# Second attention of a two-layer kernel: which turned tiles travel through DRAM, and in which order the tiles of a chunk are made and read

## The chip, the cores and the metric

The kernel runs on one core of one Trainium2 chip. The metric is the device time of one execution in microseconds; the time given is the median of several executions. One execution was also taken with the hardware profiler, and every duration below comes from that one.

## The reference

The input `x` is 8 x 128 x 48 x 48 in float32: 8 images, 128 channels, N = 48 x 48 = 2304 positions, which are the tokens.

```python
x = x + conv_attn(group_norm(x))                 # first attention, masked
t = to_tokens(x)                                  # 8 x 2304 x 128
t = t + full_attn(layer_norm(t))                  # second attention
t = t + ffn(layer_norm(t))                        # batch norm, recurrent scan
```

The first attention projects `x` and 32 channels of position encodings to `q`, `k` and `v` (a leaky ReLU each), multiplies with a lower triangular mask, takes the softmax, and multiplies with `v`. The second has no projections. With `h = layer_norm(t)` it is

```python
attn = softmax(h @ h.T)          # 2304 x 2304 for each image
out  = attn @ h
```

so `h @ h.T` is symmetric, and the change rests on that symmetry. The last part computes `h @ W.T`, normalises it over all images and tokens, and runs `y = sigmoid(wx + y @ V.T)` along the tokens.

## The kernel before

**Tiles.** Everything is float32. The 2304 tokens of an image ("batch" below) are 18 blocks of 128, or NQ = 6 chunks of 384 = QB x 128 (QB = 3). One score tile is 128 keys by 384 queries. For each batch the kernel does the group norm, the projections (L895, L898), the first attention chunk by chunk (`Causal`: scores L1032, exponential L1034, mask on GpSimd L1037, product L1043), then the second attention chunk by chunk (`Full`). The scan (L1601) follows once, after all 8 batches.

**The second attention.** After each chunk of the first attention a small chain of steps makes the normalised tokens of that chunk: `tb` is transposed on TensorE (L953) and copied by ScalarE into `xh` (L1124), channels by tokens; `xhT` holds them tokens by channels. For chunk j, `Full` accumulates in `o` the products of all 18 blocks of the exponentials with `xhT`. By symmetry only blocks in chunks n >= j are computed. Such an item is "direct": scores on TensorE (L1269), exponential on ScalarE into `p` (L1271), product on TensorE (L1291). A block in a chunk n > j is needed again, transposed, by the later chunk n. So VectorE transposes it in squares of 32 x 32 into a tile `t` of the pool `tpool`, two buffers (L1236). When the three blocks of the pair (j, n) are there, `store` writes the tile to DRAM (`e`, four transfers on SyncE's queue, L1187), in an order that swaps the squares. `load` brings it back into `g` (one transfer on SyncE's queue, pool `gpool`, three buffers, L1179), and chunk n reads it in three "turned" items (product L1279). Inside the chunk's own three blocks the same is done with smaller tiles, "mirrored" items: `tm` is written to DRAM `m` and read back into `gm`, on GpSimd's queue (L1217, L1221; product L1287).

**The order.** `Full.items` lists the items of each chunk: the chunk's own blocks first, then direct and turned items spread evenly, the mirrored items last. In chunk 0 there are 18 direct items and no turned ones; in chunk 1 there are 15 direct and 3 turned ones, the pair (0,1); and so on. The stream of all items is fixed when the program is built. A product follows its scores LAG = 3 items later. The first three items of the first attention of batch b+1 are put among the last items of the second attention of batch b.

**The planner.** Each engine and each queue works in the order in which its instructions are written out. A planner (`Stream`, `Chain`) decides that order when the program is built. It keeps an estimated clock, and `tick` runs each step of a side chain once its estimated inputs are ready. `finish(chain)` writes out all the steps of a chain that are left, and `advance` some of them. `prefetch` writes out a load if fewer than three pairs are loaded ahead and the pair was stored some microseconds earlier, then the stores whose tile is estimated to be ready. `self.pairs` gives the order of the loads: (0,1), (0,2), (1,2), (0,3) and so on, 15 in a batch.

**The rest of SyncE's queue.** After each chunk of the second attention another chain writes the new tokens to DRAM (`t_d`, L1357), and fetches them back as `t2x` (L1361) with `scale` (L1363) for the product `wx` (L1369). The position rows `pb` (L854) and pieces for the scan (`t2l_d`, L1400) go the same way. All transfers of this queue take turns on eight semaphores, so a transfer waits until the one eight before it has landed.

Of the kernel before, what the change touches and what calls it, by code (L numbers as in the profile page):

```python
# [14 lines left out]
F32 = mybir.dt.float32  # L15
# [589 lines left out]
def fast_path(ctx: ExitStack, tc: tile.TileContext, x, pe, w_ffn, out, x_tok, w_qkv, w_pos, v_t, gamma_beta, flag):  # L605
    nc = tc.nc
    B, C, H, W = x.shape
    N = H * W
    P = 128
# [4 lines left out]
    NQ = N // QC  # L614
# [52 lines left out]
    with ExitStack() as actx:  # L667
# [335 lines left out]
        class Causal:  # L1003
# [17 lines left out]

            def begin(self, j, m, first):
                b = self.b
                if first:
                    st.finish(projected[b, j])
                    allowed[b] = j + EARLY
                    following(b)
                    if j == NQ - 1:
                        bounds(b)
                off = self.offset(j, m)  # L1030
                s = psum_s(f"s_{b}_{j}_{m}")
                nc.tensor.matmul(s[:, off:QC], keys[b][:, ts(m, P)], queries[b, j][:, off:], start=True, stop=True)  # L1032
                p = pp.tile([P, QC], F32, tag="p", name=f"p_{b}_{j}_{m}")
                nc.scalar.activation(p[:, off:], s[:, off:QC], AF.Exp, scale=SCALE)  # L1034
                ops = [("ACT", 0.16 + (QC - off) * 0.00085)]
                if m >= QB * j:
                    nc.gpsimd.tensor_mul(p[:, off : off + P], p[:, off : off + P], triu)  # L1037
                    ops.append(("POOL", 0.5))
                return p, st.then(st.spend((QC - off) * US), ops)
# [103 lines left out]
        class Full:  # L1143
# [6 lines left out]
            def __init__(self, b):  # L1150
                self.b = b
                self.tiles, self.stored, self.loaded = {}, {}, {}
                self.pairs = [(i, j) for j in range(NQ) for i in range(j)]
                self.used, self.to_store = 0, deque()

            @staticmethod
            def items():
                chunks = []
                for j in range(NQ):
                    ahead = [("direct", QB * n + g) for n in range(j, NQ) for g in range(QB)]  # L1160
                    turn = [("turned", i, g) for i in range(j) for g in range(QB)]
                    both = [((k + 0.5) / len(ahead), w) for k, w in enumerate(ahead)]
                    both += [((k + 0.5) / len(turn), w) for k, w in enumerate(turn)]
                    order_of = [w for _, w in sorted(both, key=lambda e: e[0])]
                    for own in ahead[QB - 2 :: -1]:
                        order_of.remove(own)
                        order_of.insert(0, own)
                    chunks.append(order_of + [("mirrored", g) for g in range(1, QB)])
                return listed(chunks)
# [3 lines left out]
                return max(0, m - QB * j) * P if m < QB * (j + 1) else 0  # L1173

            def load(self):
                i, j = self.pairs[len(self.loaded)]
                d, _ = self.stored[i, j]
                g = gpool.tile([P, R, QB, QB, SQ], F32, tag="g", name=f"g_{self.b}_{i}_{j}")
                nc.sync.dma_start(g.rearrange("p a j m r -> p (a j m r)"), d.rearrange("p a f -> p (a f)"))  # L1179
                self.loaded[i, j] = g  # L1180

            def store(self):
                j, n, t, at = self.to_store.popleft()
                d = dpool.tile([P, R, QB * QB * SQ], F32, tag=f"e_{j}_{n}", name=f"e_{self.b}_{j}_{n}")
                turned = d.rearrange("(b c) a f -> a c b f", b=R)
                for r in range(R):
                    nc.sync.dma_start(turned[r], t[ts(r, SQ)].rearrange("c b j m r -> c b (j m r)"))  # L1187
                self.stored[j, n] = d, max(at, st.now)

            def prefetch(self):  # L1190
                n = len(self.loaded)
                if n < len(self.pairs) and n < self.used + 3 and self.pairs[n] in self.stored:
                    if self.stored[self.pairs[n]][1] + 6.0 <= st.now:
                        self.load()
                while self.to_store and self.to_store[0][3] <= st.now:
                    self.store()

            def mirror(self, j, g, p, ready):

                b, left = self.b, QB - 1 - g  # L1200
                if g == 0:
                    self.tm = chunk_tile("tm", f"tm_{b}_{j}", bufs=1).rearrange("p (b q r) -> p b q r", b=R, q=QB)
                first = g * (QB - 1)
                nc.vector.transpose(  # L1204
                    self.tm[:, :, first : first + left, :].rearrange("p b q r -> p q b r"),
                    p[:, (g + 1) * P :].rearrange("p (q b r) -> p q b r", q=left, b=R),
                )
                at = st.then(ready, [("DVE", 0.17 + left * 0.13)])
                if g < QB - 2:
                    return  # L1210
                gm = chunk_tile("gm", f"gm_{b}_{j}", bufs=1).rearrange("p (a q r) -> p a q r", a=R, q=QB)
                self.gm = gm
                d = dpool.tile([P, R, QB * SQ], F32, tag=f"m_{j % 2}", name=f"m_{b}_{j}")
                tm = self.tm

                def out_of():
                    nc.gpsimd.dma_start(d, tm.rearrange("p b q r -> p b (q r)"))  # L1217

                def back_in():
                    for r in range(R):  # L1220
                        nc.gpsimd.dma_start(  # L1221
                            gm[ts(r, SQ)].rearrange("c a q r -> c a (q r)"), d.rearrange("(a c) b f -> b c a f", a=R)[r]
                        )

                self.moved = st.add([(out_of, 0.0, [("POOL", 1.2), ("", 3.0)]), (back_in, 0.0, [("POOL", 5.0), ("", 3.0)])], at + 0.6 - st.now)
# [18 lines left out]
            def begin(self, j, what, first):  # L1244
# [10 lines left out]
                if what[0] == "turned":  # L1255
                    i, g = what[1:]
                    while (i, j) not in self.loaded:
                        while self.pairs[len(self.loaded)] not in self.stored:
                            self.store()
                        self.load()  # L1260
                    return self.loaded[i, j][:, :, g, :, :].rearrange("p a m r -> p m a r"), 0.0
# [12 lines left out]
            def product(self, j, what, o, p, ready, first, last):  # L1274
                xhT = x_hat[self.b][0]
                if what[0] == "turned":
                    i, g = what[1:]
                    out_ap = o[:, :QC].rearrange("p (m a r) -> p m a r", m=QB, a=R)
                    nc.tensor.matmul(out_ap, xhT[:, QB * i + g, :], p, start=first, stop=last)  # L1279
                    if g == QB - 1:  # L1280
                        self.used += 1
                    cols = QC
                elif what[0] == "mirrored":
# [15 lines left out]
            def after(self, j, o):  # L1299
# [126 lines left out]
                else:  # L1426
                    steps = [
                        (turn_root, 0.0, [("DVE", 0.15)]),
                        (spread, 0.0, [("", 13.0)]),
                        (fetch, 0.0, [("", 9.0)]),  # L1430
                        (product, QC * US, [("DVE", 1.0)]),
                        (stored, 0.0, [("ACT", 0.85)]),
                    ]
# [31 lines left out]
        LAG = 3  # L1465
        stream = []
        for b in range(B):
            part, items = Causal(b), Causal.items()
            if b:

                for k in range(QB):
# [216 lines left out]
```

## Time and profile before

| what | value |
|---|---|
| time, median of 3 | 1742.51 us (1737.38 to 1744.68) |
| the profiled execution | 1747.17 us |
| its span | 1745.5 us |
| TensorE busy | 1705.2 us, 98% |
| VectorE, ScalarE, GpSimd busy | 1190.0, 699.5, 453.9 us |
| moved by DMA | 278.54 MB, 160 GB/s on the mean |
| granted TensorE clock, mean | 0.995 of full |

A row of the groups or of the timeline names engine, line, operation and `out<-in` with the names of the tiles; "L1291 o<-p,xhT" is the product of a direct item. PE is TensorE, PEld its weight load, DVE VectorE, ACT ScalarE, POOL GpSimd, SP SyncE, and SPq the SyncE instructions that issue transfers. A bracket at the end of a row gives the idle time ahead of it and what ended it. Batch b of the second attention starts about 204 us after batch b-1.

### The profile page before, as it was taken

Reading aid. Unit: us, or ns where it says so; the run is one execution under the profiler, and the core shown is the slowest. Engines: PE = TensorE matmul, PEld = TensorE weight load, DVE = VectorE, ACT = ScalarE, POOL = GpSimd, SP = SyncE. Lnnn points to the kernel's source line nnn. Section 1 sums busy time; section 2 is a strip of 40 time slices with the busy share of each in tenths; the row PEclk is TensorE's granted clock in tenths of the full one; section 3 lists DMA queues with packets and bytes.
Section 4 is the critical chain, followed back from the end, with each engine's and each line's share of the span. In section 5 each row is a group of like instructions: output and inputs, shape, how many; then the busy total and the mean of one; then the engine's idle time right before and its main releaser. Section 6 shows DMA issues by size and latency. Waiting matters only on the chain.

```text
span 1745.5 us, 22358 instructions
## 1 busy us (share of the span) xinstructions
PE 1705.2 (98%) x6338; PEld 1094.7 (63%) x6339; DVE 1190.0 (68%) x3259; ACT 699.5 (40%) x1332; POOL 453.9 (26%) x637
## 2 busy tenths in 40 slices
PE   9999999999999999999999999999999999999986
PEld 6666666666666666666666666666666666666565
DVE  5865578656876478755786568864787656864457
ACT  3344334443344423443344433444244432444345
POOL 1232123311233112321224112332123212241206
PEclk9999999999999999999999999999999999999998
DMA  3317763378424874178632784338831686127858
GB/s 120 114 31 213 227 191 100 106 204 235 145 71 138 226 232 112 49 204 230 199 100 81 200 242 144 100 111 230 242 114 55 183 239 198 52 84 205 229 208 219
DMA packets 214697, 278.54 MB, mean 160 GB/s; under 512 B 93889, under 2 KB 178786, under 8 KB 214052
## 3 DMA queue, kind: packets, MB, share of 16 engines
q1 hardware_dynamic: 204396, 255.11, 50.0%
q0 software_dynamic: 9936, 21.51, 4.4%
q8 instruction: 52, 0.85, 0.2%
q14 instruction: 81, 0.66, 0.1%
q10 hardware_dynamic: 232, 0.40, 0.1%
HBM read 157.31 MB, written 119.61 MB: 159 GB/s over the span
## 4 chain that ended last, share of the span: by engine, by line
PE 89%; DMA 5%; DVE 2%; POOL 1%; SPq 1%; issue 1%; ACT 0%; POOLq 0%; DVEq 0%; ACTq 0%
PE s L1032 17%; PE o L1043 17%; PE s L1269 16%; PE o L1291 16%; PE o L1279 10%; DMA g<-e 3%; PE pj L895 3%; PE z L1601 2%; PE o L1287 2%; PE wx L1369 2%; DMA t2x<-t_d 1%; PE pj L898 1%; POOL gm L1221 1%; PE tb L953 1%; PE of_t L953 1%; SPq L1187 1%
## 5 line engine op out<-in xcount | busy, mean ns | idle before, releaser
L1271 ACT ACTIVATE p<-s,shift 128x384 f32<-128x384 f32 (+2 forms) x504 | 274.8, 551 | 544.5 <-PE s L1269 480.1
L1034 ACT ACTIVATE p<-s 128x384 f32<-128x384 f32 (+2 forms) x504 | 230.2, 460 | 395.3 <-PE s L1032 331.2
L1043 PE MATMUL o<-p,vT 128*128 128x384 f32 (+2 forms) x1008 | 377.8, 456 | 4.6 <-POOL p L1037 4.6
L1032 PE MATMUL s<-q,k 128*128 128x384 f32 (+2 forms) x1008 | 381.4, 460 | 0.1
L1269 PE MATMUL s<-xh 128*128 128x384 f32 (+2 forms) x1008 | 378.3, 457 | 0.0
L1291 PE MATMUL o<-p,xhT 128*128 128x384 f32 (+2 forms) x1008 | 367.6, 456 | 0.0
L1279 PE MATMUL o<-g,xhT 128*128 128x384 f32 x720 | 277.7, 489 | 9.7 <-DMA g<-e 9.7
L1236 DVE STREAM_TRANSPOSE t<-p 128x384 f32<-128x384 f32 x360 | 183.9, 550 | 146.3 <-DMA e<-t 75.0
L1291 PEld LDWEIGHTS o<-p,xhT 128*128 128x128 f32 x1008 | 189.2, 190 | 118.8 <-ACT p L1271 0.3
L1043 PEld LDWEIGHTS o<-p,vT 128*128 128x128 f32 x1008 | 186.7, 190 | 115.8 <-POOL p L1037 8.9
L1269 PEld LDWEIGHTS s<-xh 128*128 128x128 f32 x1008 | 184.9, 190 | 105.9
L1032 PEld LDWEIGHTS s<-q,k 128*128 128x128 f32 x1008 | 179.3, 190 | 86.5 <-issue 2.2
L1058 DVE TENSOR_TENSOR acc<-acc,p 128x384 f32<-128x384 f32 (+2 forms) x408 | 209.7, 514 | 26.7 <-DVE acc L1058 1.6
L1279 PEld LDWEIGHTS o<-g,xhT 128*128 128x128 f32 x720 | 131.6, 191 | 89.8 <-DMA g<-e 14.5
L1037 POOL TENSOR_TENSOR p<-p,triu 128x128 f32<-128x128 f32 x144 | 72.2, 505 | 288.7 <-ACT p L1034 287.9
L1221 POOL DMA_DIRECT2D gm<-m x192 | 107.4, 564 | 71.5 <-PE s L1269 25.1
L1128 POOL TENSOR_SCALAR xhT<-xhT 128x384 f32<-128x384 f32 x48 | 57.4, 1195 | 242.4 <-PE tb L953 242.4
L1343 POOL TENSOR_TENSOR roots<-ve_f,mhalf 128x3 f32<-128x3 f32 x48 | 42.3, 880 | 254.8 <-DVE ve_f L937 254.6
L1217 POOL DMA_DIRECT2D m<-tm x48 | 28.9, 602 | 205.4 <-DVE tm L1204 205.0
L1370 DVE TENSOR_TENSOR scale<-wx,scale 128x384 f32<-128x384 f32 x46 | 25.6, 557 | 78.9 <-PE wx L1369 62.9
L895 PE MATMUL pj<-xn,wT 128*128 128x384 f32 x192 | 77.9, 488 | 1.5 <-DVE xn L888 1.5
L902 DVE TENSOR_TENSOR q<-pj,pb 128x384 f32<-128x384 f32 x48 | 26.7, 556 | 69.4 <-PE pj L895 69.4
(248 smaller groups left out, 1732.9 us busy)
## 6 DMA issues: line engine op xcount, KB each, us to landing
e<-t SPq DMA_DIRECT2D x480, 144.0 KB
g<-e SPq DMA_DIRECT2D x120, 576.0 KB
pb<-posb_d SPq DMA_DIRECT2D x42, 576.0 KB
t1t<-in_x_tok_dram SPq DMA_DIRECT2D x48, 192.0 KB
m<-tm POOLq DMA_DIRECT2D x48, 192.0 KB, 4.7
gm<-m POOLq DMA_DIRECT2D x192, 48.0 KB, 3.4
t_d<-tt SPq DMA_DIRECT2D x184, 48.0 KB
t2x<-t_d SPq DMA_DIRECT2D x46, 192.0 KB
```

Source lines behind the costliest of these rows:

```text
L895: nc.tensor.matmul(ps[:, :QC], wT[:, j, :], xn, start=True, stop=True)
L1032: nc.tensor.matmul(s[:, off:QC], keys[b][:, ts(m, P)], queries[b, j][:, off:], start=True, stop=True)
L1034: nc.scalar.activation(p[:, off:], s[:, off:QC], AF.Exp, scale=SCALE)
L1037: nc.gpsimd.tensor_mul(p[:, off : off + P], p[:, off : off + P], triu)
L1043: nc.tensor.matmul(o[:, off:QC], vals[b][:, ts(m, P)], p[:, off:], start=first, stop=last)
L1058: nc.vector.tensor_add(a[:, off:], a[:, off:], p[:, off:])
L1221: nc.gpsimd.dma_start(gm[ts(r, SQ)].rearrange("c a q r -> c a (q r)"), d.rearrange("(a c) b f -> b c a f", a=R)[r])
L1236: nc.vector.transpose(t[:, :, :, g, :].rearrange("p b j r -> p j b r"), p.rearrange("p (j b r) -> p j b r", j=QB, b=R))
L1269: nc.tensor.matmul(s[:, off:QC], xh[:, ts(m, P)], xh[:, j * QC + off : (j + 1) * QC], start=True, stop=True)
L1271: nc.scalar.activation(p[:, off:], s[:, off:QC], AF.Exp, bias=shift)
L1279: nc.tensor.matmul(out_ap, xhT[:, QB * i + g, :], p, start=first, stop=last)
L1291: nc.tensor.matmul(o[:, off:QC], xhT[:, what[1], :], p[:, off:], start=first, stop=last)
```

## The change

1. The pair (j, j+1), three blocks that only the next chunk reads, no longer goes through DRAM. `store` moves its tile `t` straight into a tile `near` in sixteen transfers from SBUF to SBUF on SyncE's queue, one for each of the 4 x 4 squares of partitions and columns (32 partitions, 1152 B each). There is one `near` tile. `near_left` counts the products that still have to read it, and `prefetch` stops at a further near pair until they are written out.
2. `self.pairs` holds only the pairs (i, j) with i < j - 1, 10 a batch, and `fetched` counts their loads.
3. In `items` the direct blocks of chunk j are made in the order j, j+2, j+3, ..., and j+1 last. The turned items of chunk j stay in the order 0, 1, ..., j-1, so the near pair (j-1, j) is read last of them; in chunk 1 it is the only one.
4. The tile `tm` shares the buffers of the tag "ta" and `gm` those of the tag "toc". At j = 0 the first step that is left of the last chunk's normalising chain is written out before `tm`.
5. The first attention of batch b+1 begins with `st.finish(self.behind.moved)`: the loads of `gm` of batch b, on GpSimd's queue, are written out ahead of the first masks.
6. The planner counts 11 instead of 9 us for the fetch of `t2x` and `scale`.

The number of TensorE matmuls stays as it was. On SyncE's queue there are 80 x 4 stores instead of 120 x 4, 80 loads instead of 120, and 40 x 16 near transfers. The later lines move by up to 26: the turned product L1279 is L1301 after the change.

```diff
@@ Causal.begin
+                if first and b and j == 0:
+                    st.finish(self.behind.moved)
...
@@ Full.__init__
-                self.pairs = [(i, j) for j in range(NQ) for i in range(j)]
-                self.used, self.to_store = 0, deque()
+                self.pairs = [(i, j) for j in range(NQ) for i in range(j - 1)]
+                self.used, self.to_store, self.fetched = 0, deque(), 0
+                self.near_left = 0
@@ Full.items
-                    ahead = [("direct", QB * n + g) for n in range(j, NQ) for g in range(QB)]
+                    ahead = [("direct", QB * n + g) for n in [j, *range(j + 2, NQ), *range(j + 1, NQ)[:1]] for g in range(QB)]
@@ Full.store
                 j, n, t, at = self.to_store.popleft()
+                if n == j + 1:
+                    assert not self.near_left
+                    self.near_left = QB
+                    g = self.loaded[j, n] = work1.tile([P, R, QB, QB, SQ], F32, tag="near", name=f"near_{self.b}_{j}")
+                    for r in range(R):
+                        for k in range(R):
+                            nc.sync.dma_start(
+                                g[ts(k, SQ), r].rearrange("c j m r -> c (j m r)"), t[ts(r, SQ), k].rearrange("c j m r -> c (j m r)")
+                            )
+                    return
@@ Full.prefetch
                 while self.to_store and self.to_store[0][3] <= st.now:
+                    j, n = self.to_store[0][:2]
+                    if n == j + 1 and self.near_left:
+                        break
                     self.store()
@@ Full.mirror
                 if g == 0:
-                    self.tm = chunk_tile("tm", f"tm_{b}_{j}", bufs=1).rearrange("p (b q r) -> p b q r", b=R, q=QB)
+                    if j == 0:
+                        st.advance(normed_chunks[b, NQ - 1], 1)
+                    self.tm = chunk_tile("ta", f"tm_{b}_{j}", bufs=1).rearrange("p (b q r) -> p b q r", b=R, q=QB)
...
-                gm = chunk_tile("gm", f"gm_{b}_{j}", bufs=1).rearrange("p (a q r) -> p a q r", a=R, q=QB)
+                gm = chunk_tile("toc", f"gm_{b}_{j}", {}, 0, bufs=1).rearrange("p (a q r) -> p a q r", a=R, q=QB)
@@ Full.begin, a turned item
                     while (i, j) not in self.loaded:
-                        while self.pairs[len(self.loaded)] not in self.stored:
+                        if j == i + 1:
+                            self.store()
+                            continue
+                        while self.pairs[self.fetched] not in self.stored:
@@ Full.product, a turned item
-                    if g == QB - 1:
+                    if j == i + 1:
+                        self.near_left -= 1
+                    elif g == QB - 1:
                         self.used += 1
@@ the fetch of t2x and scale
-                        (fetch, 0.0, [("", 9.0)]),
+                        (fetch, 0.0, [("", 11.0)]),
@@ the stream
+            behind = stream[-1][0] if b else None
             part, items = Causal(b), Causal.items()
+            part.behind = behind
```

## The prediction, made before the changed kernel had run

> **What bounds the kernel now.** I read the page first: which engine has no idle time, and what the chain of waits says about it.
>
> ```profile
> PE 1705.2 (98%) x6338; PEld 1094.7 (63%) x6339; DVE 1190.0 (68%) x3259; ACT 699.5 (40%) x1332; POOL 453.9 (26%) x637
> PE 89%; DMA 5%; DVE 2%; POOL 1%; SPq 1%; issue 1%; ACT 0%; POOLq 0%; DVEq 0%; ACTq 0%
> e<-t SPq DMA_DIRECT2D x480, 144.0 KB
> g<-e SPq DMA_DIRECT2D x120, 576.0 KB
> ```
>
> TensorE is busy for 98% of the span, and the change neither adds nor removes a matmul. So it can only move the little time in which TensorE waits. The list of waits says who releases it:
>
> ```profile
> PE o L1279 <- DMA g<-e: 9.7, 12, 3.4
> PE o L1043 <- POOL p L1037: 4.6, 7, 0.7
> ```
>
> The columns are total, number and longest. These count idle time only. Measured as start-to-start gaps beyond the usual 0.645 us of a 128x384 matmul, the first group is 5.93 us in batches 0 to 6 and 5.81 us in the last, where 1.48 us at a lowered clock follow; the second is 7 x 0.83 = 5.8 us. All of it together is 19.0 us: no cure of these two waits can bring more than that, 1% of the time.
>
> Next, the end of chunk 0 and the start of chunk 1 in batch 1, on the timeline (start, duration, engine):
>
> ```profile
> 337.37 0.49 PE L953 MATMUL tb<-ident,xhT 128*128 128x128 f32 x3
> 337.89 0.48 ACT L1124 COPY xh<-tb 128x384 f32<-128x384 f32 x1 [0.39 <-PE tb L953]
> ...
> 341.57 0.81 PE L1269 MATMUL s<-xh 128*128 128x384 f32 x2
> 345.22 1.50 DVE L1236 STREAM_TRANSPOSE t<-p 128x384 f32<-128x384 f32 x3 [3.27 <-DMA e<-t]
> ...
> 349.98 0.81 PE L1279 MATMUL o<-g,xhT 128*128 128x384 f32 x2
> ```
>
> TensorE's slots are fixed by the order written out, one per 0.645 us. Chunk 0's last scores sit at about 341.57 and the first turned product of chunk 1 at 349.98, so 8.4 us lie between the last thing made in chunk 0 and the first turned tile that chunk 1 reads. Before, that tile's pair (0,1) was made first in chunk 0 and had the whole chunk for its way through DRAM. Now it is made last.
>
> Last, SyncE's queue, for what an issue costs and what stands in line ahead of chunk 5:
>
> ```profile
> 363.30 1.88 SPq L1357 DMA_DIRECT2D t_d<-tt  x4
> ...
> 402.72 3.25 SPq L1400 DMA_DIRECT2D t2l_d<-t2c  x1
> 406.73 1.93 SPq L1187 DMA_DIRECT2D e<-t  x4
> 411.71 3.12 SPq L1179 DMA_DIRECT2D g<-e  x2
> 422.31 0.34 SPq L1179 DMA_DIRECT2D g<-e  x1
> 423.56 0.34 SPq L1361 DMA_DIRECT2D t2x<-t_d  x1
> 425.69 3.52 SPq L1187 DMA_DIRECT2D e<-t  x4
> 429.93 5.39 SPq L1179 DMA_DIRECT2D g<-e  x2
> ```
>
> One issue costs 1.88 / 4 = 0.47 us for a 48 KB transfer and 1.93 / 4 = 0.48 us for a 144 KB one; a single one that follows a pause costs 0.34 us. The size hardly matters, the number does. A 48 KB transfer on an empty queue landed 1.67 us after its issue by its semaphore update, a 144 KB one 2.4 to 2.7 us, a 576 KB one 4.4 to 6.3 us.
>
> **The change part by part.** The profiled execution took 1747.17 us (span 1745.5 and 1.67 around it), 4.66 us over the median of 1742.51; the terms below are differences and are put on both.
>
> *Fewer bytes through DRAM.* 40 pairs lose four stores and one load each: 160 + 40 = 200 issues and 47 MB of transfers go. 40 x 16 = 640 issues of 36 KB, 24 MB, come. SyncE has 440 issues more, 440 x 0.47 = 207 us or 26 us per batch, beside TensorE and free, except where a wait for SyncE decides. There are two such places.
>
> *Pair (0,1), made last.* The last scores of chunk 0 start near 341.57; by the term on chunk 0's order below they are 1.3 us later; the exponential and the DVE transpose, 0.55 us each, and the hand-overs end at 345.4. Then 16 issues on SyncE: the last starts at 345.4 + 15 x 0.47 = 352.5 and lands 1.9 us later, at 354.4. The matmul in slot 349.98 + 1.3 = 351.3 needs all sixteen. Stall: about 3.0 us in each of 8 batches, 24 us. Nothing else covers it, since TensorE is in order and the two items ahead are already counted. An SBUF to SBUF transfer of 32 partitions isn't in the trace. Bounds: 0.34 us an issue gives 0.9 us, 0.47 us and a landing of 2.7 us with a slow hand-over gives 4.5 us. I take the 48 KB row, the nearest in size.
>
> A rule speaks to this. The Trainium skill, page "DMA: Bandwidth & Descriptors", section "Issuing engines are not separate DMA queues", says that the time to start a transfer is usually small beside the transfer itself; its "Rules for kernel authors" ask to merge transfers under 64 KB. In the rows above 16 issues take 7.5 us and one landing 1.7 to 2.7 us, so the first doesn't hold here. By it the pair would land near 347.9, there would be no stall, and the forecast would be 24 us lower.
>
> *Chunk 0's order 2, 3, 4, 5, 1.* Blocks of chunks 4 and 5 are wanted three matmuls sooner. Their inputs come from the transposes at 337.37 and the ScalarE copy after it, 0.48 us plus 0.39 us of hand-over. In the order of the changed kernel's TensorE stream the scores of block 12 stand only 0.45 us behind their transposes and those of block 15 directly behind, so TensorE waits for the copies: about 0.45 + 0.85 = 1.3 us a batch, 10.4 us. Bounds 0.5 and 2 us.
>
> *The load of pair (3,5), behind 16 issues.* It is read at 436.28 and was late already, by 0.4 to 1.3 us in most batches:
>
> ```profile
> 436.28 0.91 PE L1279 MATMUL o<-g,xhT 128*128 128x384 f32 x2 [0.33 <-DMA g<-e]
> ```
>
> Now it is queued behind the near transfer of chunk 4. Walk SyncE: after the write of t2l (402.72 + 3.25 = 406.0) the near transfer of chunk 3 takes 16 x 0.47, to 413.5. Then t2x, scale, the loads of (0,5), (1,5) and pb go out, to 416, 2.1 MB that land by about 424 at the 235 GB/s seen here (3.26 MB between 422.31 and 436.23). The load of (2,5) waits for that landing, since each transfer on this queue waits for the one eight before it. The near transfer of chunk 4 then waits, in its fifth to eighth issue, for these loads (to about 431.8), and its other half takes 3.8 us, to 435.6. The load of (3,5) is issued at 436.0 and lands 4.4 us later, at 440.4; its slot is 435.1. Stall 5.3 us in batches 0 to 6, 37.1 us. Bounds: 1.5 us, if the near transfer starts as soon as its tile is free (424.6) and is not held by landings, and 7 us. The last batch has this wait now and keeps it (5.9 against 5.81, taken as equal).
>
> *The clock.* The one long wait in the trace shows what follows it:
>
> ```profile
> 1662.90 1.50 PE L1279 MATMUL o<-g,xhT 128*128 128x384 f32 x2 [3.43 <-DMA g<-e]
> 1663.00:1666.50 3.50, 3.50 (x8) 2.14 (x9) 0.14 (x1) 0.00 (x0) 0.00 (x0) 0.51 0.61 225
> ```
>
> The second line is the stretch behind it; the granted clock is the column ahead of the last two, 0.51. It costs 0.64 + 0.64 + 0.20 = 1.5 us in matmuls at half pace. A stall of 2.09 us at 837.46 dropped no clock. So the 5.3 us stalls bring 7 x 1.5 = 10.5 us more. The 3.0 us ones lie between the two rows, a little nearer to 3.60; as no shorter wait in the trace dropped the clock I take none, and keep 8 x 1.5 = 12 us as the bound.
>
> *What is gained.* The waits for g in batches 0 to 6 go, or are in the term above: 5.93 us. The masks of the next batch no longer queue behind four loads of GpSimd:
>
> ```profile
> 441.96 0.70 PE L1043 MATMUL o<-p,vT 128*128 128x256 f32 x2 [0.66 <-POOL p L1037]
> 439.16 2.25 POOL L1221 DMA_DIRECT2D gm<-m  x4 [0.21 <-PE o L1279]
> 441.44 0.87 POOL L1037 TENSOR_TENSOR p<-p,triu 128x128 f32<-128x128 f32 x2
> ```
>
> The masks at 441.44 start when the loads end. With the loads ahead of the first mask, 7 x 0.83 = 5.8 us go. What is late next is the landing of m, 4.7 us after its issue: if it isn't there, the first mask waits with the loads. Bounds for this edit: 5.8 us gained, 7 x 2 = 14 us lost; I take the gain, because the late load of (3,5) leaves the masks time. Sharing the buffers "ta" and "toc" is taken at nothing: DVE has 32% idle, and the mirrored tiles are dead by the time the residual chain wants them; without that cover it would be one more wait of a microsecond a chunk.
>
> Sum: 24 + 10.4 + 37.1 + 10.5 - 5.9 - 5.8 = 70.3 us. The profiled execution would take 1817.5 us, a median 1812.8, said as 1813.
>
> **Rivals.**
>
> *Only pair (0,1) binds.* The load of (3,5) goes out before the near transfer is held up, 1.5 us late as now and without a drop of the clock. Then 24 + 10.4 + 7 x 1.5 - 11.7 = 33 us with the middle values, or 21 us with a near stall of 1.5 us: 1764 to 1776. For it speaks that 23 MB less pass the queues, so landings come sooner than in the rows I used.
>
> *Faster.* The sixteen small transfers are issued in up to 0.27 us each: (351.3 - 1.9 - 345.4) / 15 = 0.27. Then pair (0,1) lands in its slot, the queue is past chunk 4 by 431, and all late loads vanish: 1742.5 - 19.0 = 1723.5. Chunk 0's order would have to cost nothing as well. Against it, no issue on SyncE shorter than 0.30 us is in the trace.
>
> *Worse.* The near transfers of chunks 1 to 3 push t2x and scale, whose reader stalled 0.2 to 1.5 us five times before, and the clock drops after pair (0,1) as well: 70 + 12 + some 30 us, 1855.
>
> *No change.* The small gains meet a near stall at its low bound: 8 x 0.9 + 8 x 0.5 - 11.7 is nought.
>
> **How the numbers follow.** Forecast 0.62, only pair (0,1) 0.19, worse 0.07, no change 0.05, faster 0.07. The time is the forecast's, 1813. The forecast's own range, with the near stall at 1.5 to 4 us and that of (3,5) at 3 to 6.5, is 1780 to 1840. To hold 8 in 10 it reaches down to the second case, 1757, and up towards the fourth, 1846. Half a per cent is 8.7 us, what a measurement here can tell from no change. Faster 0.07, same 0.05, slower 0.88.
>
> **What would show it.** In the profile after: a wait of PE's L1301 (the old L1279) for the near transfer, 8 times about 3 us, three items into chunk 1; waits of L1301 for g of pair (3,5) near 5 us with half clock behind; PE's scores waiting for ACT's copy of xh in chunk 0; no wait of L1043 for the mask. TensorE's busy share falls from 98% to 94%. I am wrong if the near row shows issues under 0.3 us or no wait at pair (0,1), or if the wait for (3,5) stays near 1 us.

## The result, and the profile after

The changed kernel takes 1939.28 us (median of 4, 1936.74 to 1941.47), the kernel before 1742.65 us (median of 4). The ratio is 1.1115, 95% interval 1.1085 to 1.1146: 196.6 us slower. I had forecast slower, by 70 us, and a range up to 1846 us. The direction held and the size did not, by nearly a factor of three.

The lines of the page that answer to those shown before:

```profile
span 1939.5 us, 22981 instructions
PE 1757.6 (91%) x6339; PEld 1115.5 (58%) x6339; DVE 1192.4 (61%) x3259; ACT 699.2 (36%) x1332; POOL 456.3 (24%) x637
PE 66%; SPq 16%; DMA 11%; DVE 4%; issue 2%; ACT 1%; POOL 0%; DVEq 0%; POOLq 0%; ACTq 0%
e<-t SPq DMA_DIRECT2D x320, 144.0 KB
g<-e SPq DMA_DIRECT2D x80, 576.0 KB
near<-t SPq DMA_DIRECT2D x640, 36.0 KB
```

Two numbers split the loss. TensorE's idle time is span less busy: 1939.5 - 1757.6 = 181.9 us, where it was 1745.5 - 1705.2 = 40.3 us, so 141.6 us of the loss is waiting. Its busy time grew by 1757.6 - 1705.2 = 52.4 us with the same matmuls: they ran more slowly. In the chain SPq has 16% instead of 1%. SPq is SyncE while it starts transfers, not while data move. The share of DMA, transfers on their way, rose from 5% to 11%.

The list of TensorE's waits (total, number, longest) names who released it:

```profile
PE o L1301 <- DMA g<-e: 72.0, 8, 9.7
PE o L1301 <- DMA near<-t: 69.7, 20, 8.0
PE s L1291 <- ACT xh L1126: 6.2, 15, 0.6
PE pj L895 <- DVE xn L888: 7.9, 7, 1.8
```

The waits for the mask (4.6 us before) are gone. The timeline of batch 2 shows both large ones, first the near transfer of pair (0,1) and its reader, then the near transfer of chunk 4 and the load of (3,5) behind it:

```profile
598.77 10.07 SPq L1194 DMA_DIRECT2D near<-t  x16
610.29 1.62 PE L1301 MATMUL o<-near,xhT 128*128 128x384 f32 x2 [5.01 <-DMA near<-t]
...
698.09 11.56 SPq L1194 DMA_DIRECT2D near<-t  x16
709.75 0.53 SPq L1183 DMA_DIRECT2D g<-e  x1
713.73 1.65 PE L1301 MATMUL o<-g,xhT 128*128 128x384 f32 x2 [9.20 <-DMA g<-e]
```

Sixteen issues take 10.07 us, 0.63 us each. The last of them lands 1.84 us after its start by its semaphore update. I had 0.47 and 1.9 us. After both waits the clock is down, as the windows behind them show (granted clock third from the end):

```profile
610.30:613.80 3.50, 3.50 (x9) 2.44 (x10) 1.36 (x6) 0.00 (x0) 0.00 (x0) 0.50 0.00 0
713.80:717.30 3.50, 3.50 (x6) 1.98 (x7) 0.00 (x0) 0.54 (x2) 0.00 (x0) 0.50 0.67 196
```

### The profile page after: what moved, and what is told of

Read it like the earlier page. It is cut to its first block, busy times and chain, and to the rows that moved or that the text cites. A ratio compares the mean times of both kernels' runs of the same rounds, so it can differ in the third digit from the quotient of the medians.

```text
span 1939.5 us, 22981 instructions
## 1 busy us (share of the span) xinstructions
PE 1757.6 (91%) x6339; PEld 1115.5 (58%) x6339; DVE 1192.4 (61%) x3259; ACT 699.2 (36%) x1332; POOL 456.3 (24%) x637
## 4 chain that ended last, share of the span: by engine, by line
PE 66%; SPq 16%; DMA 11%; DVE 4%; issue 2%; ACT 1%; POOL 0%; DVEq 0%; POOLq 0%; ACTq 0%
PE s L1034 15%; PE o L1045 15%; SPq L1194 13%; PE s L1291 9%; PE o L1315 9%; PE o L1301 7%; DMA g<-e 3%; DMA t2x<-t_d 3%; PE pj L895 2%; PE z L1627 2%; PE wx L1393 2%; SPq L1201 1%; DMA e<-t 1%; DMA pb<-posb_d 1%; DMA near<-t 1%
## 5 line engine op out<-in xcount | busy, mean ns | idle before, releaser
L1291 PE MATMUL s<-xh 128*128 128x384 f32 (+2 forms) x1008 | 385.5, 465 | 6.2 <-ACT xh L1126 6.2
L1315 PE MATMUL o<-p,xhT 128*128 128x384 f32 (+2 forms) x1008 | 372.2, 459 | 0.0
L1301 PE MATMUL o<-g,xhT 128*128 128x384 f32 x480 | 188.9, 512 | 72.0 <-DMA g<-e 72.0
L1301 PE MATMUL o<-near,xhT 128*128 128x384 f32 x240 | 107.3, 533 | 70.5 <-DMA near<-t 69.7
L1039 POOL TENSOR_TENSOR p<-p,triu 128x128 f32<-128x128 f32 x144 | 77.1, 539 | 392.3 <-ACT p L1036 392.1
L1301 PEld LDWEIGHTS o<-g,xhT 128*128 128x128 f32 x480 | 91.6, 201 | 125.9 <-DMA g<-e 73.6
L1301 PEld LDWEIGHTS o<-near,xhT 128*128 128x128 f32 x240 | 45.1, 203 | 104.4 <-issue 71.7
L1130 POOL TENSOR_SCALAR xhT<-xhT 128x384 f32<-128x384 f32 x48 | 63.1, 1314 | 150.1 <-PE tb L953 149.9
```

Of the source, the lines that this page charges most:

```text
L1291: nc.tensor.matmul(s[:, off:QC], xh[:, ts(m, P)], xh[:, j * QC + off : (j + 1) * QC], start=True, stop=True)
L1315: nc.tensor.matmul(o[:, off:QC], xhT[:, what[1], :], p[:, off:], start=first, stop=last)
```

## The experiments

Twelve kernels ran. "Before" is given anew where a number needs it, since each group of runs had its own runs of it, between 1741.8 and 1746.8 us. Waits per batch are start-to-start gaps of TensorE beyond the usual ones. In the expectations, "theory" is what I held and "rival" the other account that the run could show.

### Four transfers instead of sixteen

```diff
-                    for r in range(R):
-                        for k in range(R):
-                            nc.sync.dma_start(g[ts(k, SQ), r]..., t[ts(r, SQ), k]...)
+                    for r in range(R):
+                        nc.sync.dma_start(g[ts(r, SQ)]..., t[ts(r, SQ)]...)
```

> The changed kernel, with the same order, the same bytes of the near pairs (576 KB from SBUF to SBUF each) but in 4 transfers of 144 KB instead of 16 of 36 KB; the squares aren't swapped between the quarters of partitions, so this kernel leaves that part of the computation out. Theory (the number of issues is the cost, 0.63 us each): near takes 4 x 0.6 = 2.4 us and lands about 4.9 us after its start instead of 12, so the wait at pair (0,1) goes (slot 6.3 us after the start), (3,5) is issued near 700.5 and lands on time, the waits at near of chunks 1 and 3 go: about 1939 - 180 = 1760 us. Rival (the bytes or the place in the order are the cost): the waits shrink by less than a third, over 1880 us.

Measured: 1733.31 us, ratio to before 0.9958 (0.9941 to 0.9975). The same bytes in the same place of the order, and 206 us less than the changed kernel, where 180 were expected. TensorE's list of waits has almost nothing left of g and near:

```profile
PE s L1290 <- ACT xh L1126: 6.2, 15, 0.6
PE o L1300 <- DMA g<-e: 2.2, 2, 1.2
PE o L1300 <- DMA near<-t: 0.4, 1, 0.4
```

SyncE's row for one pair in it:

```profile
553.06 2.47 SPq L1193 DMA_DIRECT2D near<-t  x4
```

A transfer of 144 KB costs SyncE 2.47 / 4 = 0.62 us, one of 36 KB cost 10.07 / 16 = 0.63 us. So a start costs the same for either size, and four pieces instead of sixteen bring the whole loss back. By itself this run does not tell the starts from the moving, because its pieces are also larger and stay in their quarter of the partitions. The run with every second transfer on GpSimd, below, does: it moves the same sixteen pieces as the change, starts them from two engines, and wins 186 us. Four transfers that swap the squares as well were not run.

### Chunk 0 in the old order

```diff
-for n in [j, *range(j + 2, NQ), *range(j + 1, NQ)[:1]] for g in range(QB)]
+for n in ([j, *range(j + 2, NQ), *range(j + 1, NQ)[:1]] if j else range(NQ)) for g in range(QB)]
```

> The changed kernel (1939 us), with chunk 0 alone in the old order 0, 1, 2, 3, 4, 5, so that pair (0,1) is made first again and its sixteen transfers have the whole chunk. Theory (the place: the pair is made last and read 8 us later, while sixteen issues at 0.63 us take 10 us): the wait for near at the first turned item of chunk 1 (about 5.2 us a batch), the half clock after it (about 2.6 us) and the two waits for the copy of xh (1.1 us) vanish: 8 x 8.9 = 71 us less, about 1868 us. Rival (the sixteen small transfers are slow wherever they stand, because the queue is full): they delay the stores and loads behind them, and less than 30 us are won, over 1909 us.

Measured: 1938.63 us, ratio 1.1134 (1.1095 to 1.1172): nothing won. The time is the rival's, the mechanism is neither's. The wait at pair (0,1) is gone in every batch, and another has come. First TensorE's list of waits, then the DVE and PE rows of batch 2's chunk 0:

```profile
PE tb L953 <- DVE xhT L948: 29.5, 8, 4.6
PE o L1301 <- DMA near<-t: 28.4, 13, 6.7
```

```profile
593.95 1.50 DVE L1255 STREAM_TRANSPOSE t<-p 128x384 f32<-128x384 f32 x3 [5.97 <-DMA near<-t]
595.37 0.82 DVE L948 TENSOR_SCALAR xhT<-t1t,mv_c,rs_c 128x128 f32<-128x128 f32 x3
...
595.82 0.75 PE L953 MATMUL tb<-ident,xhT 128*128 128x128 f32 x3 [3.82 <-DVE xhT L948]
```

The tile `t` is the source of the sixteen transfers, so it is given back only when the last has landed, 11 us after the first issue. `tpool` has two buffers, VectorE needs the next one and stands for 5.97 us, and the normalising of the last chunk is queued behind it on the same engine. Neither theory nor rival had said this: with the place put right, what counted was how long sixteen issues hold the tile. The waits for xn, gn_mv and p together are 15 us longer too; what makes them so is not shown.

### The load of (3,5) ahead of the near transfer

```diff
-                    if n == j + 1 and self.near_left:
+                    if n == j + 1 and (self.near_left or (j == NQ - 2 and self.fetched < len(self.pairs))):
                         break
```

> The changed kernel, with one line more: the near transfers of chunk 4 are written out only after the load of pair (3,5). Theory (the load of (3,5) is late because 16 issues stand ahead of it): issued near 698.1 instead of 709.75 in batch 2 it lands by about 703 for a slot at 704.4, so the wait of 9.2 us and about 2.7 us at half clock go; the near pair (4,5) then lands about 711.5 for a slot near 710.3, a new wait of about 1.2 us. 8 x 10.7 = 85 us less, about 1855 us. Rival (the load is late because its buffer or the data ahead of it on the queue come late): its landing moves by less than 3 us and at most 25 us are won, over 1914 us.

Measured: 1874.81 us, ratio 1.0762 (1.0721 to 1.0804): 64 us less than the changed kernel, where 85 were expected.

```profile
PE o L1301 <- DMA g<-e: 4.0, 4, 1.7
PE o L1301 <- DMA near<-t: 80.2, 27, 7.7
```

The waits for g fall from 72.0 to 4.0 us: the load was late because of the issues ahead of it. The near pair (4,5) is now late by 15.5 us over 8 batches, where 8 x 1.2 = 10 us were allowed for; the rest of the missing 21 us is not accounted for.

### Dummy products in the two long waits

```diff
+                    if g == 0 and (i, j) in ((0, 1), (NQ - 3, NQ - 1)):
+                        idle(psum_s(f"fill_{self.b}_{j}"), 22 if j == 1 else 38)
                     nc.tensor.matmul(out_ap, xhT[:, QB * i + g, :], p, start=first, stop=last)
```

> The changed kernel, with dummy products of the identity (128x128) on TensorE just ahead of the two products that wait longest: 22 of them before the first read of pair (0,1), 38 before the first read of pair (3,5), in every batch, no other change. They fill the wait and nothing more. Theory (both waits are followed by a stretch at half clock, since TensorE stood still): the waits stay as long as they are, the half clock behind them goes, 8 x (2.6 + 2.7) = 42 us less, about 1897 us, granted clock above 0.98. Rival (the 52 us more of busy time of TensorE have another cause, as reads that compete with the small transfers): time within 8 us of 1939, or longer.

Measured: 1917.54 us, ratio 1.1011 (1.0960 to 1.1062): 21.7 us less than the changed kernel, against 42 expected and under 8 by the rival. The windows behind the filled waits of batch 2 are at full clock:

```profile
605.00:608.50 3.50, 3.34 (x15) 2.36 (x16) 2.13 (x9) 0.58 (x1) 0.00 (x0) 1.00 0.00 0
705.70:709.20 3.50, 3.48 (x11) 2.16 (x12) 0.56 (x2) 1.52 (x2) 0.45 (x1) 1.00 0.63 186
```

So standing still is what lowers the clock there. What it costs can be estimated from start-to-start gaps inside the stretches at half clock. In the changed kernel the matmuls there start 46 us later in all than at the usual pace, 36 us of it behind the two waits that were filled and 9 us behind those at near of chunk 3. In the filled kernel it is 16 us: 2 us behind the two places, and 12 us at near of chunk 3. So the slow matmuls behind the two waits are as good as gone, but only 22 of these 34 us come out as time. Waits elsewhere grew: those at near of chunk 1 are 11.2 us instead of 5.7. What makes up the rest is not shown.

### The order alone, through DRAM

The kernel before, with the diff's line of `items` and nothing else:

```diff
-                    ahead = [("direct", QB * n + g) for n in range(j, NQ) for g in range(QB)]
+                    ahead = [("direct", QB * n + g) for n in [j, *range(j + 2, NQ), *range(j + 1, NQ)[:1]] for g in range(QB)]
```

> The kernel before, with another part alone: the blocks for chunk j+1 are made last in chunk j, as in the change, but their pair still goes through DRAM in 4 stores and 1 load. By the rows, pair (0,1) then needs 1.9 us for the stores, 2.6 us to land and 4.3 us for the load, 8.8 us, against 12 us for the sixteen direct transfers, and its slot comes 6.3 us after its tile is ready. Theory (what costs is the number of issues): the wait at pair (0,1) is 2.5 to 3.5 us, shorter than the 5.2 us of the change, with little half clock behind it, and the two waits for xh of 1.1 us are there; 8 x 5 = 40 us more than before, about 1783 us. Rival (the place at the end is the cost, whichever way the tile takes): the wait is as long as in the change or longer, over 5 us, and the time is over 1850 us.

Measured: 1768.94 us, ratio 1.0155 (1.0126 to 1.0184), 26 us more than before, 14 less than expected, and 170 less than the change.

```profile
PE o L1279 <- DMA g<-e: 24.6, 16, 2.6
```

The wait at pair (0,1) is 2.63 us in batch 2 (1.7 to 2.7 us over the batches), half of that with the direct transfers. The detour through DRAM, four stores and a load, is sooner there than the direct way in sixteen pieces.

### The mirrored loads ahead of the masks, alone

The kernel before, with this part of the diff and nothing else:

```diff
@@ Causal.begin
+                if first and b and j == 0:
+                    st.finish(self.behind.moved)
@@ the stream
+            behind = stream[-1][0] if b else None
             part, items = Causal(b), Causal.items()
+            part.behind = behind
```

> The kernel before, with one part of the change alone: the loads of gm of batch b are written out ahead of the first masks of batch b+1 on GpSimd. Theory (part of the forecast, not touched by what went wrong): the seven waits of TensorE for a mask of 0.83 us each go, 5.8 us less, 1736 us. Rival (the first mask then waits behind the landing of m, 4.7 us after its issue): up to 14 us more, 1756 us, with waits of TensorE for the mask of 1 to 2 us.

Measured: 1749.84 us, ratio 1.0029 (1.0010 to 1.0047): 7 us slower, neither the 5.8 us gain nor the rival's wait at the mask. TensorE's list:

```profile
PE o L1289 <- DMA gm<-m: 6.0, 1, 6.0
PE s L1271 <- ACT xh L1126: 4.0, 7, 0.6
PE tb L953 <- DVE xhT L948: 2.6, 7, 0.6
PE o L1281 <- DMA g<-e: 6.2, 4, 2.4
```

The waits for the mask are gone, as forecast, and those for g fall from 9.7 to 6.2 us. In their place come waits for `tb` and `xh` in chunk 0, 1.1 to 1.6 us in each of the seven batches that have the edit, and one for gm of 6.0 us, where it was 1.9. `finish` moves the planner's clock on to the chain's estimated end, and from there on the written order of other steps differs too. That this shift makes the new waits was not tried apart.

### Every second transfer on GpSimd

```diff
-                            nc.sync.dma_start(
+                            (nc.sync if (r + k) % 2 else nc.gpsimd).dma_start(
                                 g[ts(k, SQ), r]...
```

> The changed kernel, with every second of the sixteen near transfers issued by GpSimd instead of SyncE. Theory (SyncE's issues in a row are the cost): a pair then takes 8 x 0.63 = 5.1 us to issue and lands about 7 us after its start; the wait at pair (0,1) falls from 5.2 to about 1 us, those at near of chunks 1 and 3 go, the load of (3,5) waits 5 us less and still is 4 us late: about 8 x 15 = 120 us less, 1820 us. Rival (the sixteen transfers themselves hold each other up on the engines that move them): the last landing moves by less than 2 us, and the time stays over 1900 us.

Measured: 1753.31 us, ratio 1.0064 (1.0040 to 1.0089), 186 us less than the changed kernel, more than the 120 expected. The GpSimd row of pair (0,1) in batch 2:

```profile
553.45 3.99 POOL L1194 DMA_DIRECT2D near<-t  x8 [6.12 <-DVE t L1255]
```

GpSimd starts one of them in 0.50 us, SyncE in 0.63. The load of (3,5) is 0.5 us late in batch 2, where I expected 4: with half the issues on it, SyncE's queue is no longer behind when chunk 5 comes.

### Three repairs together, in two forms

First form: the three edits above on the changed kernel, that is, chunk 0 in the old order, the load of (3,5) first, and every second transfer on GpSimd.

> The changed kernel with three repairs together: chunk 0 in the old order, the load of (3,5) ahead of the near transfer of chunk 4, and every second near transfer issued by GpSimd. Theory: with half the issues on SyncE the tile of pair (0,1) is given back to VectorE some 5 us sooner, so the wait of VectorE that ate the gain of the old order in chunk 0 shrinks from 6 to about 1 us; the waits for near and g are all under 1 us. About 1742 us, even with before; from 1733 us, where the four-transfer kernel is, to 1755 us. Rival (GpSimd's issues come late or hold up its masks and its loads of gm): new waits of TensorE for masks or gm of over 1 us a batch, over 1765 us.

Measured: 1777.98 us, ratio 1.0201 (1.0180 to 1.0223), worse than the split alone. TensorE waits for the normalising again, and the GpSimd rows of batch 2 tell why:

```profile
PE tb L953 <- DVE xhT L948: 24.6, 8, 4.0
```

```profile
545.27 3.97 POOL L1194 DMA_DIRECT2D near<-t  x8
549.23 2.20 POOL L1240 DMA_DIRECT2D gm<-m  x4
551.44 0.90 POOL L943 TENSOR_TENSOR rs_c<-ve_c,mhalf 128x3 f32<-128x3 f32 x1
```

`rs_c`, the root that the normalising needs, is queued on GpSimd behind twelve issues. The rival had named masks and gm; it was the root.

Second form: chunk 0 in another order.

```diff
-... if j else range(NQ)) for g in range(QB)]
+... if j else [0, 2, 3, 4, 1, 5]) for g in range(QB)]
```

> The changed kernel with three repairs: every second near transfer issued by GpSimd, the load of (3,5) ahead of the near transfer of chunk 4, and chunk 0 in the order 0, 2, 3, 4, 1, 5, so that pair (0,1) is made three blocks (3.9 us) sooner than in the change but not so soon that its tile or GpSimd's issues hold up the normalising of chunk 5. Theory: the waits for near and g, 0.6 and 0.5 us a batch and 5.1 and 3.1 us in the last batch with the split alone (1753 us), go, and half of the waits for xh: 1753 - 8 x 1.6 - 8 = 1732 us, from 1725 to 1740. Rival (as with chunk 0 in the old order, a wait of the normalising takes their place): waits of tb for VectorE of over 2 us a batch, over 1760 us.

Measured: 1741.95 us, ratio 1.0000 (0.9984 to 1.0016): even with before, 10 us more than expected. Pair (0,1) is still late, by 0.4 to 1.5 us in most batches, and the loads of gm are late in four places:

```profile
PE o L1311 <- DMA gm<-m: 5.9, 4, 2.6
```

The longest of these waits is in batch 3. The GpSimd rows ahead of it:

```profile
809.05 0.57 POOL L1236 DMA_DIRECT2D m<-tm  x1 [3.65 <-DVE t L1255]
...
815.56 2.24 POOL L1240 DMA_DIRECT2D gm<-m  x4 [5.04 <-issue]
818.95 3.94 POOL L1194 DMA_DIRECT2D near<-t  x8 [1.16 <-DMA e<-t]
```

The loads wait until the store of m has landed, 5.9 us after its start, and no near issue stands between the two. Why that landing is late is not shown.

### The same without the masks edit

```diff
-                if first and b and j == 0:
-                    st.finish(self.behind.moved)
```

> The kernel of the run with three repairs, without the part that writes the loads of gm out ahead of the first masks. Theory (that part costs more than it brings, by the 7 us that it cost alone, because the planner's clock jumps with it and later steps are written out nearer to their readers): 5 to 8 us faster than with it, the waits for the mask of 0.8 us in seven batches back, those of chunk 0 for tb and xh gone. Rival (with the other parts the loads find their data and the part brings its 5.8 us): 4 to 7 us slower than with it.

Measured: 1750.99 us, ratio 1.0054 (1.0035 to 1.0073). The time is the rival's: with the other repairs the masks edit is worth 9 us, though it costs 7 alone. The rival's mechanism is not seen. In the profile of the kernel without the edit TensorE never waits for a mask, so no 5.8 us came back; what it lists instead are waits for gm and for gn_m, the product of the group norm:

```profile
PE o L1309 <- DMA gm<-m: 7.7, 9, 1.2
PE gn_m L809 <- DVE gn_mv L803: 3.6, 6, 0.8
```

The two profiled executions, 1751.05 us with the edit and 1751.90 us without, are too close to show the 9 us of the medians. What makes the difference stays open.

### The same with all sixteen on SyncE

```diff
-                            (nc.sync if (r + k) % 2 else nc.gpsimd).dma_start(
+                            nc.sync.dma_start(
```

> The kernel of the run with three repairs, with all sixteen near transfers on SyncE again. Theory (16 x 0.63 us on one queue against the time to the reader): pair (0,1) starts 3.9 us sooner, so its wait is 5.2 - 3.9 = 1.3 us, with no half clock; near of chunks 1, 3 and 4 stay late by 0.4, 1.6 and 1.9 us with 1 to 2 us of waits for t2x and xn behind them: with the 1875 us of the kernel with the load moved, 8 x (3.9 + 2.2) = 49 us less, about 1826 us; from 1790 us if the queue runs ahead as a whole. Rival (the tile of pair (0,1), held for 12 us, stops VectorE as in the old order): waits of tb of over 3 us and over 1850 us.

Measured: 1852.55 us, ratio 1.0629 (1.0600 to 1.0658), against 1826 expected and at the rival's bound. The waits for near are 62.0 us in 25 places, but there is none of over 0.3 us for `tb`, so it is not the rival's mechanism. The wait at pair (0,1) is 3.4 to 4.3 us a batch, where 1.3 were expected. In batch 2 its near transfer starts 8.8 us ahead of the slot instead of 6.3; of the 3.9 us that the earlier block should give, 1.4 are lost because VectorE stood for a buffer that the stores had not yet given back:

```profile
570.31 1.50 DVE L1255 STREAM_TRANSPOSE t<-p 128x384 f32<-128x384 f32 x3 [3.00 <-DMA e<-t]
```

Beside the kernel with three repairs this is the price of SyncE's sixteen issues in a repaired order: 111 us.

### Over three queues

```diff
-(nc.sync if (r + k) % 2 else nc.gpsimd).dma_start(
+(nc.sync, nc.gpsimd, nc.sync, nc.scalar, nc.gpsimd, nc.sync, nc.gpsimd, nc.scalar)[(R * r + k) % 8].dma_start(
```

> The kernel with three repairs (1742 us), with the sixteen near transfers over three queues: six on SyncE, six on GpSimd, four on ScalarE. Theory (what is left is still the time to start the transfers): a pair starts in 3.8 us instead of 5.1, the waits at pair (0,1) of 0.4 to 1.5 us a batch go, and GpSimd reaches its loads of gm 1 us sooner, so their waits of 6.9 us in all halve: 1742 - 7 - 3.5 = 1731 us, which would beat the kernel before by 0.6%. Rival (four issues of 0.6 us on ScalarE hold up the exponentials, whose products follow three items later): waits of TensorE for p, 1745 us or more.

Measured: 1845.71 us, ratio 1.0572 (1.0550 to 1.0595). The rival is right that TensorE now waits for p, but the price is far above what I thought. The rows of the three queues for pair (0,1) in batch 2, and ScalarE's next exponentials:

```profile
570.25 1.55 POOL L1194 DMA_DIRECT2D near<-t  x3 [2.97 <-DVE t L1255]
571.17 2.46 ACTq L1194 DMA_DIRECT2D near<-t  x4
573.73 1.52 ACT L1293 ACTIVATE p<-s,shift 128x384 f32<-128x384 f32 x3 [2.42 <-DMA near<-t]
574.28 5.50 SPq L1194 DMA_DIRECT2D near<-t  x6
```

Three exponentials stand behind four issues of 0.6 us. By the list of ScalarE's waits it stands 60.9 us in all behind near transfers. TensorE waits 18.3 us for p, but also 34.6 for g and 19.0 for near. One link to these two is in the trace: ScalarE's transfers take turns on the same eight semaphores as SyncE's. SyncE's first near transfer uses the semaphore of the one that ScalarE started at 571.17; that one landed at 574.2, and SyncE started at 574.28, 4 us after GpSimd. SyncE's list of waits has

```profile
SPq L1201 <- DMA near<-t: 96.2, 36, 4.7
```

and in the kernel with three repairs it has no wait behind near transfers at all. How much of the 104 us goes this way is not shown. No version with the squares swapped beat the kernel before.

## Why the prediction was wrong, by its own steps

| term | forecast, us | measured, us |
|---|---|---|
| pair (0,1), 8 batches | 24 | 45.3 (5.0 to 5.7 each, 8.1 in batch 0) |
| load of (3,5), batches 0 to 6 | 37.1 | 63.5 (8.5 to 9.6 each) |
| the same in the last batch | 0 | 4.1 (9.9 against 5.8) |
| near of chunks 1 and 3 | 0 | 29.0 (5.7 and 23.3) |
| chunk 0's order | 10.4 | 9.0 (0.40 + 0.73 a batch) |
| matmuls at a lower clock | 10.5 | 52.4 (growth of busy time) |
| gains (g, masks) | -11.7 | -11.7 |

The measured terms are sums of start-to-start gaps; the last but one is from the busy times. Together they make 191.6 of 196.6 us, and waits for xn grew by 6.4 us.

**The step that failed is the price of one issue.** I took 0.47 us from the 48 KB transfers to DRAM, "the nearest in size", and kept 0.34 us as a lower bound and nothing above 0.47. Size was the wrong likeness, as the rows that I quoted said themselves: "the size hardly matters". From SBUF to SBUF one costs 0.63 us, in 36 KB and in 144 KB alike. With 0.63 the steps as written give 345.4 + 15 x 0.63 + 1.9 = 356.8 against a slot at 351.3, a wait of 5.5 us (measured 5.0 to 5.7), and for (3,5), which has two near transfers ahead of it in my walk, 5.3 + 2 x 16 x 0.16 = 10.4 us (measured 8.5 to 9.6). So these two mechanisms were right, and one price entered sixteen-fold, twice. That it is the two ends in SBUF which set the price, and not something else that the near transfers have in common, was not tried apart. The rate of 235 GB/s in the walk was read too low (the profile gives 260 for 422.31 to 436.23), which moves the walk by less than 1 us.

**Two terms at nothing followed from it.** The near transfers of chunks 1 and 3 come late by 0.3 to 1.2 us and by 1.6 to 3.9 us in batches 0 to 6. Sixteen issues at 0.16 us more are 2.6 us for each of them, about what it takes; with four issues the waits are all but gone. The 7.1 us of chunk 3 in the last batch are more than this explains. I had these transfers only in the case "worse", and there as a delay of t2x and scale.

**The clock** was the second largest miss: 42 us, against 81 us in the first four rows of the table, which go back to the issues. The waits at pair (0,1) passed the 3.60 us row because of the issue price. But my reading that no shorter wait in the trace dropped the clock was wrong by that trace itself. Just ahead of the scan TensorE stood for 1.33 and 0.62 us, and the clock fell to half:

```profile
1676.75:1680.16 3.41, 1.75 (x7) 1.06 (x8) 0.86 (x3) 0.70 (x2) 1.12 (x2) 1.00 0.64 175
1680.16:1683.57 3.41, 3.35 (x18) 3.08 (x17) 2.56 (x6) 1.76 (x2) 0.56 (x1) 0.50 0.94 392
```

The last section says what decides. I had also priced each drop at 1.5 us; behind the waits for (3,5) the half clock lasts 6.8 or 10.2 us, part of it while TensorE still waits.

**What held.** The two places and the waits' names; the waits for the copy of xh, 1.13 us against 1.3; the masks' waits gone in the changed kernel, though in the kernel with three repairs they are gone without the edit as well; the case "faster" only if issues cost 0.27 us, of which the four-transfer kernel, which leaves the swap out, is the counterpart: with a quarter of the issues it does win, 0.4%.

The Trainium skill's page "DMA: Bandwidth & Descriptors", section "Issuing engines are not separate DMA queues", says that the time to start a DMA is usually small beside the DMA itself. I set this against sixteen starts and one landing, which is not what it compares. For one transfer a start is a third of the way to the landing here, 0.63 against 1.84 us. What the sentence leaves out is that the starts of one engine follow each other while the landings overlap: sixteen starts take 10.07 us, and the last landing comes 1.84 us after the last start.

## What to carry to other kernels

Count transfers before bytes: price a new kind of transfer by the row with the same ends (SBUF or DRAM), not the same size, and when no row has them, let the bound go above the nearest row too. A transfer also holds its source tile until it has landed, and its start holds whatever stands behind it on the issuing engine; sixteen short ones held the tile for 11 us here. Moving some to another engine helped where little that somebody waits for was queued on it (GpSimd, 186 us won, until `rs_c` stood behind its issues), and cost 104 us where the exponentials were (ScalarE).

## What the runs showed of the hardware that I had not expected

SyncE takes 0.63 us to start a transfer from SBUF to SBUF, 0.47 to 0.48 us from SBUF to DRAM and 0.34 to 0.53 us for a load; GpSimd takes 0.50 us for the same SBUF to SBUF transfer, ScalarE 0.6 us.

The clock falls after waits well below the 3.60 us of the row before, but not after all of them. What decides is where the wait lies. In every profile of this case the granted clock changes on a fixed grid of 3.41 us (in the kernel before it halves at 1663.10 and at 1680.16, five steps apart), and it halves when TensorE was busy for too little of the step just ended. In the changed kernel TensorE stood idle for 2.09 us until 457.41, all within one step. The rows are three steps; the first number after the length is TensorE's busy time, the granted clock is third from the end:

```profile
454.48:457.89 3.41, 1.32 (x5) 0.49 (x3) 1.69 (x4) 0.17 (x1) 0.00 (x0) 1.00 0.46 112
457.89:461.30 3.41, 3.22 (x10) 1.94 (x9) 0.00 (x1) 1.13 (x1) 0.00 (x0) 0.50 0.71 159
461.30:464.71 3.41, 3.41 (x15) 2.30 (x15) 3.34 (x7) 1.75 (x3) 0.00 (x0) 1.00 1.00 403
```

In the kernel before it stood idle for 1.93 us until 837.46 (2.09 us from start to start, the row that my prediction went by). There the edge of a step, at 837.07, cuts the wait in two:

```profile
833.66:837.07 3.41, 1.88 (x7) 0.94 (x5) 2.85 (x8) 1.06 (x2) 0.40 (x2) 1.00 0.77 200
837.07:840.48 3.41, 3.02 (x12) 2.23 (x13) 0.28 (x1) 1.52 (x2) 0.24 (x1) 1.00 0.95 290
```

Busy for 1.32 of 3.41 us, 39%, the clock halved in the next step; busy for 1.88, 55%, it did not. In the kernel with the order alone a longer idle time, 2.47 us until 562.07, was cut at 560.43 and left the steps 76% and 52% busy: no drop. In all fourteen profiles together, from 20 us after the start on (ahead of that the clock also fell after busier steps), all 114 steps at full clock in which TensorE was busy for less than 41% were followed by one at half clock, 16 of the 62 between 41% and 55%, and none of the 6951 above. These shares go by the profile's busy times, in which the ends of matmuls are modelled; what decides between 41% and 55% is open.
